# A two-layer transformer block on one core: feed-forward rests of two steps together, keys before queries at the start, normalised tokens written by GpSimd

## The chip, the cores and the metric

The kernel runs on one core of a Trainium2 chip. The core has a matrix engine (TensorE; PE for its matmuls and PEld for its weight loads in the profile), VectorE (DVE), ScalarE (ACT), GpSimd (POOL) and SyncE (SP), which here only issues DMAs. Each engine works through its own instructions in order and waits on semaphores for the others. Matmuls write PSUM, of which a core has eight banks of 128 rows by 512 float32; TensorE, VectorE and ScalarE reach PSUM here, and GpSimd works in SBUF.

The metric is the device time of one execution in microseconds (us). The kernel before takes 3205.06 us, the median of three runs (3204.47 to 3205.57).

## The reference

Two layers of the same form work on `x`, 4 batch elements of 512 tokens with 320 features, all in float32. Each layer has self-attention, attention to a context of 1601 tokens with 192 features, and a gated feed-forward, each with a layer norm ahead of it and a residual sum behind it:

```
def _ln(x, g, b):
    m = jnp.mean(x, axis=-1, keepdims=True)
    v = jnp.mean(jnp.square(x - m), axis=-1, keepdims=True)
    return (x - m) * jax.lax.rsqrt(v + EPS) * g + b
...
h1 = _ln(x, n1_g, n1_b)
x = _attn(h1, h1, q1, k1, v1, o1_w, o1_b, heads) + x
h2 = _ln(x, n2_g, n2_b)
x = _attn(h2, context, q2, k2, v2, o2_w, o2_b, heads) + x
h3 = _ln(x, n3_g, n3_b)
proj = h3 @ ff_w1 + ff_b1
a, g = jnp.split(proj, 2, axis=-1)
ff = a * jax.nn.gelu(g, approximate=False) @ ff_w2 + ff_b2
return ff + x
```

Attention has 20 heads of 16 features. The feed-forward's inner width is 1280, so `ff_w1` has 2560 columns: 1280 for `a`, 1280 for the gate `g`.

## The kernel before

**Units.** The work is a list of 88 units, in this order for each layer: 20 units of self-attention (4 batch elements times 5 groups of 4 heads), 20 of attention to the context, and 4 of feed-forward (one a batch element). Scores are computed turned, keys on partitions and 512 queries along the free dimension (`st`, line 1074); ScalarE takes the exponential (L1080); a second matmul multiplies by values and a column of ones (`av`, L1094). ScalarE copies that to SBUF (`vo`, L1110) and GpSimd adds it to the group's sum `o` (L1111). Each unit's softmax needs a maximum per query and head first; that is taken one unit ahead, by matmuls into `sps` (L903) and reduces on VectorE (`nmax`, `pm`, L919). Maxima are turned and sent by eight small DMAs into spare rows of the queries (`max_end`, L974).

**What sets the order.** The program is written out by hand in one order, which each engine keeps. Beside the fixed loops there are chains of small pieces of work ("norm", "proj", "values", "project" and others), each with an estimated cost, a due round and conditions. In every round a planner (`steps`, `pick`, `pace`) takes pieces whose turn has come and places them behind the fixed work of that round. `run(chain)` places the next piece of a chain at once, and `until(test, chain)` places pieces until something holds.

**Layer norm.** `add_norm` is a chain of pieces. Statistics are taken on VectorE (L468, L469). A reciprocal root is found by a guess and three refinements on tiny tiles, on VectorE while `start["on"]` holds, which is at the first norm alone, and on GpSimd afterwards (L438, L445 to L448). `normalise(t)` writes (x - mean) * root for one tile of 128 tokens into `hn` (L484): 320 elements a row and, ahead of a feed-forward, 64 more as a second instruction. At least one round later `turn(k)` transposes `hn` with TensorE (`hps`, L497), ScalarE writes `hT` with scale and bias, and GpSimd adds the next residual's bias to `x` (L510). There are 24 norms; 23 come after the start.

**Projections.** A self-attention unit has one piece of queries (`qps`, L699) and one of keys (`kps`, L725), 24 short matmuls each. For the first unit, ScalarE and VectorE write the result straight from PSUM into slots of 32 rows (L641, L643). For later ones ScalarE copies it (L711, L737) and GpSimd writes the slots (L647), four instructions a piece. Values (`vps`, L830) are made in eight pieces for a batch element, four of 128 columns and four of 192.

**PSUM.** `ps_st` has four single banks (tag `st`), `ps_m` two pairs of banks (tag `m`). A tile of a pool waits until an earlier tile's readers are done.

**Feed-forward.** `ff_main` (L1170) goes through ten chunks of 128 inner features, two chunks a step, five steps (c = 0, 2, 4, 6, 8). For each chunk there is a bank for `a` (from `ps_st`) and one for the gate (a half of a `ps_m` tile). The contraction over 320 is split in two of 128 rows, `full` (L1194), and a rest of 64, `rest` (L1206). The rests of `a` use rows 0 to 63 of the array and those of the gate rows 64 to 127. A float32 matmul appears as two PE instructions. At the end of a step, `gate` has ScalarE take the gelu (L1212) and VectorE the product into `hid` (L1213). `beside` gives maxima of the next unit and planned pieces their place ahead of a step and in its middle. After the five steps, `yps` (L1233) multiplies by `ff_w2`, and VectorE adds to `x`.

**Start.** Lines 1353 to 1388 load `x` and the first weights, make the first norm, project units 0 and 1, and then take the maxima of unit 0 in four rounds with pieces of values between them.

Of the kernel before, what the change touches and what calls it, by code (L numbers as in the profile page):

```python
# [66 lines left out]
def kernel(ctx: ExitStack, tc: tile.TileContext, x, context, ws, out):  # L67
# [285 lines left out]
    def add(chain, cost, f, due, ready=yes, soon=yes):  # L353
        chains[chain].append((cost if isinstance(cost, tuple) else (cost,), due, ready, soon, f))
# [69 lines left out]
    def until(test, name):  # L424
        while not test():
            assert chains[name], name
            run(name)
# [31 lines left out]
    def add_norm(l, b, i, put, done, due):  # L459
        xb = xs[b]  # L460
        s = {}

        def stats(t):
            if t == 0:
                hn_used.append(b)
                s["mv"] = two.tile([P, NQ, 2], F32, tag="mv", name="mv")
            st = three.tile([P, 6], F32, tag="st6", name="st6")
            nc.vector.bn_stats(st, xb[:, t, :])  # L468
            nc.vector.bn_aggr(s["mv"][:, t, :], st)  # L469

        def root(step):
            if step == 0:
                s["root"] = guess_root(s["mv"][:, :, 1])
                s["rstd"] = s["root"][1]
            for _ in range(step + 1):
                better_root(*s["root"])
            s["round"] = clock["round"]

        def normalise(t):
            if t == 0:  # L480
                s["hn"] = one.tile([P, NQ, D + REST], F32, tag="hn", name="hn")

            for to, at, n in ((0, 0, D), (D, D - REST, REST))[: 1 + i // 2]:
                nc.vector.tensor_scalar(  # L484
                    s["hn"][:, t, to : to + n], xb[:, t, at : at + n],
                    s["mv"][:, t, 0:1], s["rstd"][:, t : t + 1], ALU.subtract, ALU.mult,
                )
            s["round"] = clock["round"]

        def turn(k, at, n):  # L490
            if k == 0:
                s["hT"] = two.tile([P, 3, N], F32, tag="hT", name="hT")
                readers.append(done)
            ps = step_bank([P, N], "hps")
            n += REST if n == REST else 0
            for t in range(NQ):
                nc.tensor.transpose(ps[:n, t * P : (t + 1) * P], s["hn"][:, t, at : at + n], ident)  # L497
            if start["on"] and k == 1:
                nc.vector.tensor_scalar(
                    s["hT"][:n, k, :], ps[:n, :],  # L500
                    lng[i][:n, k : k + 1], lnb[i][:n, k : k + 1], ALU.mult, ALU.add,
                )
            else:
                nc.scalar.activation(
                    s["hT"][:n, k, :], ps[:n, :], AF.Identity,
                    bias=lnb[i][:n, k : k + 1], scale=lng[i][:n, k : k + 1],
                )
            for t in ((0,), (1,), (2, 3))[k]:

                nc.gpsimd.tensor_tensor(xb[:, t, :], xb[:, t, :], brow[(3 * l + i) % 2], ALU.add)  # L510
            if k == 2:
                hn_used.pop()
                put(s["hT"])

        for t in range(NQ):
            add(
                "norm", LIGHT, lambda t=t: stats(t), due - 22 + t,
                (lambda: stage[b] == 3 * l + i and not hn_used and b in loaded) if t == 0 else yes,
                (lambda: b == 0 or clock["round"] >= loaded[b] + 5) if t == 0 else yes,
            )  # L520
        for step in range(2):
            add(
                "norm", 0.0 if step else LIGHT, lambda step=step: root(step), due - 18 + step, yes,
                (lambda: clock["round"] > s["round"]) if step else yes,
            )
        for t in range(NQ):
            add(
                "norm", LIGHT, lambda t=t: normalise(t), due - 13 + t, yes,
                (lambda: clock["round"] >= s["round"] + 1) if t == 0 else yes,
            )  # L530
        for k, at, n in (DK if i < 2 else FK + [(2, 2 * P, REST)]):
            add(
                "norm", 0.58, lambda k=k, at=at, n=n: turn(k, at, n), due - 6 + 2 * k,
                may_overwrite if k == 0 else yes, lambda: clock["round"] >= s["round"] + 1,
            )
# [113 lines left out]
    def add_proj(u):  # L649
# [145 lines left out]
                add(chain, (0.05 + 0.427 / parts,) * 3, lambda part=part: queries(part), due - 2, unread)  # L795

        if not u.cross:
            add_queries()
            add(chain, (0.477,) * 3, keys, due, free)
        else:  # L800
            add(chain, 2.45, keys_of_context, keys_due, free)
            add_queries()
            for _ in range(HG):
                add(
                    "slots", 0.0, lambda: u.kslots and u.kslots.popleft()(), keys_due,
                    lambda: u.keyed, lambda: clock["slots"] > 0,
                )
# [362 lines left out]
    def ff_main(u, give, nxt):  # L1170
        done = 0

        def beside(room, n):

            nonlocal done
            if room:
                for extra in give(done, True)[1]:
                    round_of([], extra)
            done += n
            if done == u.steps - 1 and nxt is not None and nxt.kind != "ff":  # L1180
                max_reduce(nxt)
                max_end(nxt)
            steps(True)
            for _ in range(n - 1):
                steps(False)

        hc = one.tile([P, 6, N], F32, tag="ctxT", name="hid")
        hid = [hc[:, i, :] for i in range(6)]

        hid += [kbuf[1][:, i * N : (i + 1) * N] for i in range(3)] + [kbuf[2][:, :N]]  # L1190

        def full(c, i, ps):
            for k, at, n in FK:
                nc.tensor.matmul(  # L1194
                    ps,
                    lhsT=w1[:, k, i * FF + c * P : i * FF + (c + 1) * P],
                    rhs=u.hT[:, k, :],
                    start=(k == 0),
                    stop=False,
                )  # L1200
            return ps

        def rest(c, pss):
            for i, ps in enumerate(pss):
                rows = slice(i * REST, (i + 1) * REST)
                nc.tensor.matmul(  # L1206
                    ps, lhsT=w1r[rows, c * P : (c + 1) * P], rhs=u.hT[rows, 2, :], start=False, stop=True
                )

        def gate(c, pss):  # L1210
            gl = prs.tile([P, N], F32, tag="pr", name="gl")
            nc.scalar.activation(gl, pss[1], AF.Gelu, bias=b1[:, NHC + c : NHC + c + 1])  # L1212
            nc.vector.scalar_tensor_tensor(hid[c], pss[0], b1[:, c : c + 1], gl, ALU.add, ALU.mult)  # L1213

        for c in range(0, NHC, 2):

            beside(True, 2)
            gates = ps_m.tile([P, 2, 512], F32, tag="m", name="fps")
            pss = []
            for i in range(2):  # L1220
                if i:
                    beside(False, 2)
                ps = ps_st.tile([P, 512], F32, tag="st", name="fps")
                pss.append([full(c + i, 0, ps), full(c + i, 1, gates[:, i])])
            for i in range(2):
                rest(c + i, pss[i])
            for i in range(2):
                gate(c + i, pss[i])
        ff_read.append(u)
        for t in range(NQ):  # L1230
            ps = ps_st.tile([P, 512], F32, tag="st", name="yps")
            for c in range(NHC):
                nc.tensor.matmul(  # L1233
                    ps[:, :D],
                    lhsT=hid[c][:, t * P : (t + 1) * P],
                    rhs=w2[:, c, :],
                    start=(c == 0),
                    stop=(c == NHC - 1),
                )
            nc.vector.tensor_tensor(xs[u.b][:, t, :], ps[:, :D], xs[u.b][:, t, :], ALU.add)  # L1240
            if u.l == L - 1:
                dma(out=out[u.b, t * P : (t + 1) * P, :], in_=xs[u.b][:, t, :])
            beside(True, 1)
        after(u)
# [113 lines left out]
    add_norms(0)  # L1358
    add_proj(units[0])
    warm(5)  # L1360
    add_proj(units[1])
    until(lambda: not chains["proj"], "proj")
    add_values(units[0])
    add_proj(units[2])
    first = units[0]
    first.pairs = max_pairs(first)
    start["both"] = True
    while left(first):
        round_of([], first.pairs[0].popleft() + first.pairs[1].popleft())
        if left(first):  # L1370
            run("values")

    run("proj")
    run("values")
# [8 lines left out]
    start["on"] = start["both"] = False  # L1383
    run("proj")

    for _ in range(3):
        run("values")
    clock["credit"] = 0.0

# [45 lines left out]
```

## Time and profile before

| | |
|---|---|
| median of three runs | 3205.06 us |
| the profiled execution's own time | 3204.68 us |
| its span, first to last instruction | 3202.9 us |
| TensorE matmuls busy | 3167.7 us (99%) |
| VectorE busy | 2068.9 us (65%) |
| ScalarE busy | 1972.4 us (62%) |
| GpSimd busy | 1202.3 us (38%) |
| the first feed-forward, four units | from about 1330 to 1608 us |
| the second feed-forward, four units | from about 2920 to 3200 us |
| writes of `hn` on VectorE (L484) | 128, 65.1 us together |
| granted TensorE clock, mean | 0.999 of full speed |

A group's line names the source line, engine, operation, output and inputs and the shape, then the count; behind the first bar its busy time and the mean duration in ns; behind the second the idle time of the engine ahead of it and what ended most of that. A timeline's line has start and duration in us, engine, line, operation, tiles and count, and in brackets the idle time ahead of it with what ended it. The chain of waits follows the work that ended last back to the beginning. Matmuls overlap and their ends are modelled, so the starts of two blocks tell more than a block's own length.

### The profile page before, as it was taken

How to read it: one execution, taken by the hardware profiler on the slowest of the kernel's cores; microseconds unless marked ns; L12 is line 12 of the kernel's file. 1: busy time of each engine (PE TensorE's matmuls, PEld its weight loads, DVE VectorE, ACT ScalarE, POOL GpSimd, SP SyncE). 2: the span in 40 equal slices, each digit the busy share in tenths (PEclk: the TensorE clock that was granted, in tenths of full speed). 3: DMA queues.
4: the chain of work that ended last, by engine and by line, in shares of the span. 5: the costliest groups of instructions: out<-in, count | busy, mean ns of one | idle time of the engine just before them, and what ended most of it. 6: DMA issues, size and time to landing. Idle time of an engine off the chain costs nothing. (4 is left out here: it accounts for less than half of the span.)

```text
span 3202.9 us, 81370 instructions
## 1 busy us (share of the span) xinstructions
PE 3167.7 (99%) x33970; PEld 1462.6 (46%) x33970; DVE 2068.9 (65%) x2663; ACT 1972.4 (62%) x3951; POOL 1202.3 (38%) x1617
## 2 busy tenths in 40 slices
PE   8999999999999999999999999999999999999999
PEld 3444444444444444354444444444444444443555
DVE  7787778778678677422247777777777777773221
ACT  4666577777777777611146665778778777785110
POOL 5555334443443443201125553344444444432000
PEclk9999999999999999999999999999999999999999
DMA  2220011100100100100012100110010010001000
GB/s 66 56 70 17 14 27 38 33 21 20 32 21 21 31 16 11 39 6 0 1 30 61 34 14 14 24 27 16 16 32 9 16 32 11 14 10 37 9 11 15
DMA packets 104851, 77.84 MB, mean 24 GB/s; under 512 B 42908, under 2 KB 95012, under 8 KB 104484
## 3 DMA queue, kind: packets, MB, share of 16 engines
q1 hardware_dynamic: 104400, 72.63, 9.2%
q8 instruction: 268, 4.39, 0.6%
q14 instruction: 99, 0.81, 0.1%
q0 software_dynamic: 64, 0.00, 0.0%
q10 hardware_dynamic: 20, 0.00, 0.0%
HBM read 33.04 MB, written 7.93 MB: 13 GB/s over the span
## 5 line engine op out<-in xcount | busy, mean ns | idle before, releaser
L1080 ACT ACTIVATE pr<-st 128x512 f32<-128x512 f32 (+1 forms) x2720 | 1408.8, 602 | 430.1 <-PE sps L903 366.4
L1074 PE MATMUL st<-q,kT 32*128 32x512 f32 (+1 forms) x5440 | 1363.3, 614 | 3.8 <-DVE nmax L919 1.5
L919 DVE TENSOR_REDUCE pm<-sps 128x2 f32<-128x1024 f32 (+1 forms) x974 | 1133.9, 1203 | 269.0 <-PE sps L903 262.7
L903 PE MATMUL sps<-kT,q 32*128 32x512 f32 x5120 | 1273.6, 620 | 14.3 <-DVE nmax L919 11.3
L1111 POOL TENSOR_TENSOR o<-o,vo 128x512 f32<-128x512 f32 x576 | 734.3, 1275 | 1373.1 <-ACT vo L1110 1201.8
L1074 PEld LDWEIGHTS st<-q,kT 32*128 32x128 f32 (+1 forms) x5440 | 504.0, 181 | 520.0 <-ACT pr L1080 291.7
L1094 PE MATMUL av<-pr,vals 128*32 128x512 f32 (+1 forms) x5440 | 729.3, 605 | 0.2
L919 DVE TENSOR_REDUCE nmax<-sps 128x2 f32<-128x1024 f32 (+1 forms) x339 | 378.2, 1156 | 148.0 <-PE sps L903 145.9
L903 PEld LDWEIGHTS sps<-kT,q 32*128 32x128 f32 x5120 | 405.3, 183 | 125.9 <-issue 81.4
L1110 ACT COPY vo<-av 128x512 f32<-128x512 f32 x576 | 339.7, 590 | 45.5 <-PE av L1094 41.4
L1094 PEld LDWEIGHTS av<-pr,vals 128*32 128x32 f32 (+1 forms) x5440 | 110.0, 108 | 493.3 <-ACT pr L1080 480.1
L1194 PE MATMUL fps<-hT,w 128*128 128x512 f32 x640 | 288.2, 599 | 1.9 <-DVE hid L1213 1.9
L1212 ACT ACTIVATE gl<-fps,b 128x512 f32<-128x512 f32 x80 | 50.7, 684 | 386.7 <-PE fps L1206 386.7
L647 POOL TENSOR_SCALAR q<-qst,keep,zero 64x128 f32<-64x128 f32 (+1 forms) x476 | 231.1, 486 | 59.9 <-ACT qst L711 26.7
L1194 PEld LDWEIGHTS fps<-hT,w 128*128 128x128 f32 x640 | 117.4, 190 | 148.8 <-issue 142.4
L438 POOL TENSOR_SCALAR root<-root 128x4 f32<-128x4 f32 x23 | 5.3, 231 | 332.7 <-DVE root L432 332.2
L1213 DVE SCALAR_TENSOR_TENSOR hid<-fps,b,gl 128x512 f32<-128x512 f32 x48 | 33.8, 746 | 147.5 <-ACT gl L1212 147.5
L1021 PEld LDWEIGHTS ops<-wo,aT 112*32 112x32 f32 (+1 forms) x3072 | 97.8, 110 | 68.3 <-issue 37.1
L699 PE MATMUL qps<-hT,wq 112*32 112x128 f32 (+3 forms) x2880 | 125.5, 308 | 0.5 <-DVE pm L919 0.5
L1021 PE MATMUL ops<-wo,aT 112*32 112x160 f32 (+1 forms) x3072 | 125.2, 300 | 0.2
L699 PEld LDWEIGHTS qps<-hT,wq 112*32 112x32 f32 (+1 forms) x2880 | 86.3, 110 | 79.1 <-issue 38.9
L1240 DVE TENSOR_TENSOR x<-yps,x 128x320 f32<-128x320 f32 x32 | 15.7, 491 | 146.5 <-PE yps L1233 146.5
(88 smaller groups left out, 2259.6 us busy)
## 6 DMA issues: line engine op xcount, KB each, us to landing
kT<-kst SPq DMA_DIRECT2D x320, 48.0 KB
aT<-o SPq DMA_DIRECT2D x320, 32.0 KB
q<-turned SPq DMA_DIRECT2D x636, 1.0 KB
w<-in_L_xattn_ff_w_dram SPq DMA_DIRECT2D x20, 256.0 KB
ctxT<-ctxT SPq DMA_DIRECT2D x24, 208.0 KB
ctxT<-ctxT SPq DMA_DIRECT2D x12, 416.0 KB
ctxin<-in_ctx_dram SPq DMA_DIRECT2D x24, 192.0 KB
w<-in_L_xattn_ff_w_dram SPq DMA_DIRECT2D x20, 160.0 KB
```

Source lines behind the costliest of these rows:

```text
L647: nc.gpsimd.tensor_scalar(to, stage[rows, :w], keep[b][rows], more[rows], ALU.mult, ALU.add)
L699: nc.tensor.matmul(ps[to, :w], lhsT=wq[:n, k, gs], rhs=first.hT[:n, k, at[i] : at[i] + w], start=(k == 0), stop=(k == 2),)
L903: nc.tensor.matmul(ps, lhsT=u.q[j * SLOT : (j + 1) * SLOT, t * P : (t + 1) * P], rhs=u.kT[j * SLOT : (j + 1) * SLOT, u.k0 + s * 512 : u.k0 ...
L919: nc.vector.tensor_reduce(to[:, j : j + n], part, AX.X, ALU.max, negate=(ns == 1))
L1021: nc.tensor.matmul(ps[f : f + m, : D // 2], lhsT=aT[:n, k, t * P + f : t * P + f + m], rhs=wo[:n, k, cols], start=(k == 0), stop=(k == 2),)
L1074: nc.tensor.matmul(st[:r, :], lhsT=u.kT[rows, u.k0 + u.cols[c] : u.k0 + u.cols[c] + r], rhs=u.q[rows, :], start=True, stop=True)
L1080: nc.scalar.activation(p[:r], st[:r], AF.Exp)
L1094: nc.tensor.matmul(ps[i * SLOT : (i + 1) * SLOT, :], lhsT=columns_of[:r, head : head + SLOT], rhs=pr.pop((c, j))[:r, :], start=True, stop= ...
L1110: nc.scalar.copy(vo, ps)
L1111: nc.gpsimd.tensor_tensor(u.o, u.o, vo, ALU.add)
L1194: nc.tensor.matmul(ps, lhsT=w1[:, k, i * FF + c * P : i * FF + (c + 1) * P], rhs=u.hT[:, k, :], start=(k == 0), stop=False,)
L1212: nc.scalar.activation(gl, pss[1], AF.Gelu, bias=b1[:, NHC + c : NHC + c + 1])
```

## The change

There are three parts.

*Feed-forward.* `full` now does both contractions of both banks of a chunk; `rests` does the four rests of a step. In steps 0, 4 and 8 the rests follow the full matmuls, as before. Behind the rests of steps 0 and 4, the banks of the next step (2 and 6) are taken at once and that step's rests are placed there, as the first contribution to those banks. In steps 2 and 6 the full matmuls then add to banks already begun, and no rests follow. `beside` is called in the same order and with the same arguments as before. Both `ps_st` banks of a step are now taken together.

*Start.* For unit 0 the keys are placed ahead of the queries. Unit 1's projections are no longer placed ahead of the rounds of maxima but behind the first and second of them; values follow behind the third. Four pieces of values instead of three come after the start, so six in all instead of seven are placed ahead of the main loop.

*Normalised tokens.* `normalise` uses GpSimd unless `start["on"]` holds, so 23 of the 24 norms.

```diff
-                nc.vector.tensor_scalar(
+                (nc.vector if start["on"] else nc.gpsimd).tensor_scalar(
                     s["hn"][:, t, to : to + n], xb[:, t, at : at + n],
...
         if not u.cross:
-            add_queries()
+            if u.i:
+                add_queries()
             add(chain, (0.477,) * 3, keys, due, free)
+            if not u.i:
+                add_queries()
...
-        def rest(c, pss):
+        def full(c, pss, ahead):
+
             for i, ps in enumerate(pss):
-                rows = slice(i * REST, (i + 1) * REST)
-                nc.tensor.matmul(
-                    ps, lhsT=w1r[rows, c * P : (c + 1) * P], rhs=u.hT[rows, 2, :], start=False, stop=True
-                )
+                for k, at, n in FK:
+                    nc.tensor.matmul(
+                        ps,
+                        lhsT=w1[:, k, i * FF + c * P : i * FF + (c + 1) * P],
+                        rhs=u.hT[:, k, :],
+                        start=ahead and k == 0,
+                        stop=not ahead and k == 1,
+                    )
+
+        def rests(c, pss, ahead):
+
+            for e in range(2):
+                for i, ps in enumerate(pss[e]):
+                    rows = slice(i * REST, (i + 1) * REST)
+                    nc.tensor.matmul(
+                        ps,
+                        lhsT=w1r[rows, (c + e) * P : (c + e + 1) * P],
+                        rhs=u.hT[rows, 2, :],
+                        start=ahead,
+                        stop=not ahead,
+                    )
...
+        def banks():
+            gates = ps_m.tile([P, 2, 512], F32, tag="m", name="fps")
+            return [[ps_st.tile([P, 512], F32, tag="st", name="fps"), gates[:, e]] for e in range(2)]
+
+        pss = None
         for c in range(0, NHC, 2):
...
+            ahead = pss is not None
+            if not ahead:
+                beside(True, 2)
+                pss = banks()
+
+            for e in range(2):
+                if e or ahead:
+                    beside(ahead and not e, 2)
+                full(c + e, pss[e], not ahead)
+            these, pss = pss, None
+            if not ahead:
+                rests(c, these, False)
+                if c + 2 < NHC:
+                    pss = banks()
+                    rests(c + 2, pss, True)
+            for e in range(2):
+                gate(c + e, these[e])
...
     warm(5)
+    until(lambda: not chains["proj"], "proj")
     add_proj(units[1])
-    until(lambda: not chains["proj"], "proj")
     add_values(units[0])
...
-    while left(first):
+    for chain in ("proj", "proj", "values", None):
         round_of([], first.pairs[0].popleft() + first.pairs[1].popleft())
-        if left(first):
-            run("values")
+        if chain:
+            run(chain)
...
-    for _ in range(3):
+    for _ in range(4):
         run("values")
```

More of the change, by code (lines that the diff above doesn't have):

```diff
@@ L1190, in ff_main @@
         hid += [kbuf[1][:, i * N : (i + 1) * N] for i in range(3)] + [kbuf[2][:, :N]]
[L1192 to L1199, printed above, removed]
-                )
-            return ps
-        def rest(c, pss):
-            for i, ps in enumerate(pss):
-                rows = slice(i * REST, (i + 1) * REST)
-                nc.tensor.matmul(
-                    ps, lhsT=w1r[rows, c * P : (c + 1) * P], rhs=u.hT[rows, 2, :], start=False, stop=True
-                )
+        def full(c, pss, ahead):
+            for i, ps in enumerate(pss):
+                for k, at, n in FK:
[17 more added lines that the diff above has]
+                    )
         def gate(c, pss):
@@ L1213, in gate @@
             nc.vector.scalar_tensor_tensor(hid[c], pss[0], b1[:, c : c + 1], gl, ALU.add, ALU.mult)
+        def banks():
+            gates = ps_m.tile([P, 2, 512], F32, tag="m", name="fps")
+            return [[ps_st.tile([P, 512], F32, tag="st", name="fps"), gates[:, e]] for e in range(2)]
+        pss = None
         for c in range(0, NHC, 2):
[L1217 to L1228, printed above, removed]
+            ahead = pss is not None
[14 more added lines that the diff above has]
+                gate(c + e, these[e])
         ff_read.append(u)
```

## The prediction

> **What bounds the kernel now.** I read the page first: its engine shares, its slices, its chain of waits and its groups.
>
> ```profile
> span 3202.9 us, 81370 instructions
> PE 3167.7 (99%) x33970; PEld 1462.6 (46%) x33970; DVE 2068.9 (65%) x2663; ACT 1972.4 (62%) x3951; POOL 1202.3 (38%) x1617
> ...
> PE 25%; DVE 0%; POOL 0%; ACT 0%; issue 0%; ACTq 0%; DVEq 0%
> ```
>
> From the list of groups, the line that the change moves to another engine:
>
> ```profile
> L484 DVE TENSOR_SCALAR hn<-x,mv,root 128x320 f32<-128x320 f32 (+1 forms) x128 | 65.1, 547 | 15.5 <-POOL root L448 15.3
> ```
>
> The reader is to see that TensorE is busy from end to end and that the chain holds almost nothing else; work taken off VectorE counts only where TensorE waits for VectorE. The list of waits shows how rarely: TensorE's `sps` matmuls waited 11.3 us for `nmax` and 2.7 for `pm`. So a gain must be TensorE time. The merged chain, in order of time, shows the last feed-forward unit (starts, then durations in us):
>
> ```profile
> 3133.02 6.87 PE fps L1194 x16
> 3139.88 1.92 PE fps L1206 x8
> 3141.80 7.06 PE fps L1194 x16
> 3148.86 1.92 PE fps L1206 x8
> ```
>
> Sixteen full matmuls take 6.87 us after `yps` (also 128 rows high) and 7.06 after the 64-row rests: entering 128-row work from another height costs 0.2. Single full matmuls follow each other by 0.43 (the timeline's weight loads: 3.43 per 8). Two rests run at once, on rows 0 to 63 and 64 to 127, so eight should take 4 x 0.43 = 1.72; they take 1.92, another 0.2. Rests are thus already side by side in pairs; what is left is 0.2 per change of height.
>
> Next, the timeline of TensorE and VectorE around one pair of steps with other work between:
>
> ```profile
> 2947.27 1.99 PE L1206 MATMUL fps<-hT,w1r 64*128 64x512 f32 x8
> ...
> 2949.19 1.09 PE L497 MATMUL hps<-ident,hn 128*128 128x128 f32 x8
> 2949.39 1.27 ACT L1212 ACTIVATE gl<-fps,b 128x512 f32<-128x512 f32 x2 [9.82 <-PE fps L1206]
> 2950.11 1.41 DVE L1213 SCALAR_TENSOR_TENSOR hid<-fps,b,gl 128x512 f32<-128x512 f32 x2 [5.27 <-ACT gl L1212]
> ...
> 2950.92 3.70 PE L1194 MATMUL fps<-hT,w 128*128 128x512 f32 x8 [0.64 <-DVE hid L1213]
> ```
>
> Counted from the rests' start, gelu begins at +2.12, the two products end at about +3.6 and +4.25, and the next full matmul waits until +3.65 for the bank that the first product frees: the oldest of the four is taken.
>
> **The feed-forward.** Per unit five groups of rests become three: steps (0, 2) and (4, 6) share one, step 8 keeps its own: two mergers a unit, 16 in all. Each removes one entry into 64-row height (0.2) and the later return to 128 rows (0.2), unless 32-row work (`ops`, `sps`) follows there and needs its own entry. Counts of instructions stay. In the timeline, 32-row work follows step 2 or 6 at both places in the first unit of each layer, once in layer 0's second, and at both of layer 0's last: 7 of 16. So 9 x 0.4 + 7 x 0.2 = 5.0 us.
>
> The merger holds four small banks across the next step's start; that step's other work gets the two that step c's products free. The second four rests end at +3.43, plus 0.2 for a change of height, 3.63. One early transpose or projection then finds the bank freed (3.65): nothing. A second waits to 4.27. Three places have two transposes there (1358.8, 1434.2, 2949.2). Before, the fulls after them start at +3.65 with rests still to come; after, at 4.27 + 0.44 = 4.71 with the rests done: a 1.92 block less, 1.06 later, so 0.86, of which 0.2 or 0.4 is counted above: about 1.6 us for the three. In layer 0's last unit, `sps` and `kps` come there. `sps` takes both freed banks, and `kps` (at 1559.9 and 1585.1, now +3.6) must wait for VectorE: products to 4.25, a reduce of 1.2 and one of 0.6, so about +6.1. The step pair goes from 15.64 to 16.2: 0.6 lost at each, where 0.2 gained was counted, so -1.6. Together 5.0 us, bounds 2.5 and 7.
>
> **The start.** Keys, then queries of unit 0 leave by the same alternating ACT/DVE line of eight pieces (13.21 to 17.28). The first `sps` at 17.34 waited for the last, a piece of keys; with keys first it needs only the sixth (queries' first half), 1.2 us sooner. Unit 1's projections (1.5 us each on TensorE) move from 14.3 to 17.0, where TensorE waited anyway, into the gaps between rounds, in place of values of 0.87. A round is bound by reduces at 2.45, and 1.14 + 1.5 = 2.64 overruns it twice, 0.25 each. The last reduce, its transpose and the eight issues of `q<-turned` on SP, ACT and POOL move up 0.7. POOL still issues its two behind the 2.5 us of unit 2's slots (30.41); unit 1's slots, 5 us of POOL, come 1.4 later and end before. Of seven values, six are left; the other (1.18) falls after 34, where TensorE waits for reduces up to 0.75 at a time. Gain 0.7, bounds 0 and 1.2. The planner's later choices may shift by an item of work: 1.5 either way.
>
> **The normalised tokens.** 23 norms, 92 writes of 320 elements and 32 of 64, leave VectorE. No row has them on GpSimd. Nearest are its tensor-scalars with per-row operands:
>
> ```profile
> L647 POOL TENSOR_SCALAR q<-qst,keep,zero 64x128 f32<-64x128 f32 x320 | 143.8, 449 | 23.0
> L647 POOL TENSOR_SCALAR kT<-kst,keep,ones 64x256 f32<-64x256 f32 x156 | 87.6, 561 | 36.9 <-ACT kst L737 23.8
> ...
> L510 POOL TENSOR_TENSOR x<-x,brow 128x320 f32<-128x320 f32 x96 | 84.0, 893 | 62.2 <-DVE hn L484 52.1 <-DMA brow<-in_L_xattn_o_b_dram 8.2
> ```
>
> Slope 0.87 ns an element: 0.62 at 320, 0.39 at 64, so 92 x 0.62 + 32 x 0.39 = 70 us on an engine at 38%. I take 0.62; ends 0.56 (256 elements) and 0.89 (two inputs). What queues behind: `o` sums, slots of `q` and `kT`, `x + brow`. Laid onto GpSimd's timeline behind the sum of the same round, the writes push `o` by at most 0.6 us and slots by 0.7, which are read rounds later; `x + brow` by up to 3.7, hidden by the rounds before the next statistics. The root is on GpSimd already, so the hand-over that VectorE waited for (15.3) goes.
>
> Who waits is the first transpose. It has 1.1 to 12 us after the last write in attention, and GpSimd would start a write up to 5.3 later than VectorE did (2.7 in the norms with less than 2). Only at 78.5 is it late: the `o` sum ends at 78.53, two writes at 79.8, so 1.1. At 1315 and 2905, where TensorE stood at the write already, eight writes from 2901.8 end near 2905.9: 0.4 each. Loss 1.9. At 0.89 a write they become 1.6 and twice 1.5, 4.6.
>
> Against that, VectorE's write was long where it met GpSimd's sum:
>
> ```profile
> 2382.17 1.28 POOL L1111 TENSOR_TENSOR o<-o,vo 128x512 f32<-128x512 f32 x1
> 2382.25 1.73 DVE L484 TENSOR_SCALAR hn<-x,mv,root 128x320 f32<-128x320 f32 x2 [0.69 <-POOL root L448]
> 2383.91 2.34 DVE L919 TENSOR_REDUCE pm<-sps 128x2 f32<-128x1024 f32 x2
> ```
>
> The first of the two writes took 1.38 where 0.44 is usual, the reduce behind it came late, and `kps` at 2385.17 waited 0.9 for it. The like at 2617.96 costs 0.4; at 801 and 1039 `kps` waits for `ctxT` behind one and two writes, 0.3 and 0.6; near 1633 perhaps 0.3. Gain 2.5, net 0.6, bounds -2 and 3. Were the cover gone, every late microsecond would fall on TensorE's transposes.
>
> [...] The rows here say 0.62 to 0.44, a factor of 1.4. [...]
>
> **Sum.** 5.0 + 0.7 + 0.6 = 6.3. The profiled execution took 3204.68 (1.8 around its span), 0.4 under the median of 3205.06; from the median, 3198.8.
>
> **Rivals.** (1) The mergers don't save the returns: the drain between heights is paid in the rests' second half, or other work stands at more junctions. Only entries count, 16 x 0.2 = 3.2, less 1.6 for layer 0's last unit; with the rest 1.3: 3202.2. For it: 7 of 16 places have such work. Against: 6.87 after `yps`. (2) VectorE's relief is worth more. TensorE's waits for `nmax` and `pm` come to 14 us; if a third of what isn't near a write shortens as well, 4 more: 3195. Against: most lie at 298 to 400 and 1900 to 2000, with no write there. (3) Slower: two free banks are too few, because the bank taken is the last freed. Then the fulls of step c + 4 wait for the product of the pair just ended, 0.2 + 0.69 + 0.75 = 1.65 us, at 16 places: 26 us, 3225. Against: 2950.92 shows the oldest taken. From 0.4 us a place it eats the gain.
>
> **How the numbers follow.** Mine 0.58, rival 1 0.20, rival 2 0.16, rival 3 0.06. About 0.2% (6.4 us) is what a measurement can tell: the border is 3198.65, in the middle of my case (3196.5 to 3201). Half of mine and rival 2 are faster: 0.45; the other half and rival 1 same: 0.49. The range takes in half of rival 2 and rival 1 with the bad ends of its terms: 3195 to 3203.5.
>
> **What would show it.** Per feed-forward unit two blocks of 16 rest instructions (3.6 us) and one of 8; fulls after such pairs 6.87. `hn` on POOL near 0.62; `hps` waiting for it at about 78, 1315 and 2905 alone. First `sps` near 16.2, first `st` near 33.1. It is wrong if fulls or steps wait for `hid` longer than 0.8, or if `hps` waits for `hn` in many norms.

## The result and the profile after

The kernel after takes 3211.75 us (median of ten runs, 3210.23 to 3215.01), the kernel before 3205.22 in ten runs beside it (3204.47 to 3210.42). The ratio is 1.0019, with a 95% interval of 1.0011 to 1.0028: slower by 6.5 us where 6.3 of gain was forecast. The profiled execution took 3215.01 (span 3213.2), 3.3 above the median. One thing varies from execution to execution, and it is told below: where TensorE's granted clock falls to one half.

The page first: TensorE's busy time is shorter by 1.7 us, the span longer by 10.3, and GpSimd, which had 0% of the chain of waits, has 2% of it (the chain that could be followed covers some 67% of the span here, 25% before).

```profile
span 3213.2 us, 81419 instructions
PE 3166.0 (99%) x33970; PEld 1465.4 (46%) x33970; DVE 2010.3 (63%) x2539; ACT 1973.3 (61%) x3951; POOL 1348.1 (42%) x1741
...
PE 63%; POOL 2%; DVE 2%; issue 0%; ACT 0%; DMA 0%; SPq 0%; DVEq 0%; POOLq 0%; ACTq 0%
```

The groups with their shapes kept apart answer the line that the change moved. The columns behind the bar are busy time and the mean of one in ns.

```profile
L647 POOL TENSOR_SCALAR q<-qst,keep,zero 64x128 f32<-64x128 f32 x320 | 144.6, 452 | 23.0
L484 POOL TENSOR_SCALAR hn<-x,mv,root 128x320 f32<-128x320 f32 x92 | 132.4, 1442 | 1.9
...
L647 POOL TENSOR_SCALAR kT<-kst,keep,ones 64x256 f32<-64x256 f32 x156 | 87.1, 558 | 41.8 <-ACT kst L737 28.7
...
L484 POOL TENSOR_SCALAR hn<-x,mv,root 128x64 f32<-128x64 f32 x32 | 18.6, 582 | 0.0
...
L484 DVE TENSOR_SCALAR hn<-x,mv,root 128x320 f32<-128x320 f32 x4 | 1.5, 443 | 0.0
```

A write of 320 elements takes 1442 ns on GpSimd, not 620; the first norm's four, still on VectorE, take 443 (547 was VectorE's mean before, with writes that met GpSimd's sums). From 64 to 320 elements the slope is (1442 - 582) / 256 = 3.36 ns an element, where the slots of `q` and `kT` have (558 - 452) / 128 = 0.83. GpSimd is loaded with 151 us of these writes where 70 was put.

The list of waits (total, times, longest) has a new pair of lines; before, no transpose waited for GpSimd:

```profile
PEld hps L497 <- POOL hn L484: 19.0, 16, 1.8
...
PE hps L497 <- POOL hn L484: 13.5, 12, 1.6
```

The timeline at one of these places, the norm at 2157 us:

```profile
2156.47 1.28 POOL L1114 TENSOR_TENSOR o<-o,vo 128x512 f32<-128x512 f32 x1
...
2157.45 0.43 PE L497 MATMUL hps<-ident,hn 128*112 128x128 f32 x2
2157.73 2.85 POOL L484 TENSOR_SCALAR hn<-x,mv,root 128x320 f32<-128x320 f32 x2
...
2159.22 0.32 PE L497 MATMUL hps<-ident,hn 128*112 128x128 f32 x1 [1.34 <-POOL hn L484]
...
2160.64 1.32 PE L497 MATMUL hps<-ident,hn 128*112 128x128 f32 x5 [1.09 <-POOL hn L484]
```

Two of the four writes are behind an `o` sum, so the third and fourth transposes stand 1.34 and 1.09 us. That is not the whole price. The windows around it (length, busy time of PE, PEld, DVE, ACT and POOL, then the granted clock):

```profile
2157.00:2160.00 3.00, 1.20 (x11) 0.32 (x3) 1.08 (x1) 1.26 (x3) 3.00 (x3) 1.00 0.49 143
2160.00:2163.00 3.00, 2.36 (x13) 1.52 (x17) 0.00 (x0) 1.55 (x2) 3.00 (x4) 0.51 0.00 0
2163.00:2166.00 3.00, 3.00 (x20) 0.79 (x16) 1.42 (x2) 1.38 (x3) 0.46 (x1) 0.50 0.00 0
```

Behind the stall TensorE runs at half clock: in the trace's clock record for 6.83 us from 2160.04, and likewise for 6.83 from 1316.95 and 3.41 from 2917.80. At the 0.50 and 0.51 of these windows up to half of such a stretch is lost by my estimate, so up to 3.4 us at each of the first two places, more than the two stalls here together (2.43).

The feed-forward shows what the prediction said. The merged chain in its last unit (starts, then durations):

```profile
3144.09 6.87 PE fps L1199 x16
3150.95 3.63 PE fps L1212 x16
3154.59 13.93 PE fps L1199 x32
3168.52 3.63 PE fps L1212 x16
```

Sixteen rests in 3.63 us where two blocks of 1.92 stood, and 6.87 + 7.06 for the fulls on both sides of a step boundary without rests.

### The profile page after: what moved, and what is told of

It is laid out like the page before. It is cut to its first block, busy times and chain, and to the rows that moved or that the text cites. A ratio compares the mean times of both kernels' runs of the same rounds, so it can differ in the third digit from the quotient of the medians.

```text
span 3213.2 us, 81419 instructions
## 1 busy us (share of the span) xinstructions
PE 3166.0 (99%) x33970; PEld 1465.4 (46%) x33970; DVE 2010.3 (63%) x2539; ACT 1973.3 (61%) x3951; POOL 1348.1 (42%) x1741
## 4 chain that ended last, share of the span: by engine, by line
PE 63%; POOL 2%; DVE 2%; issue 0%; ACT 0%; DMA 0%; SPq 0%; DVEq 0%; POOLq 0%; ACTq 0%
PE st L1077 16%; PE av L1097 13%; PE sps L906 8%; PE fps L1199 8%; PE yps L1253 5%; PE fps L1212 2%; PE ops L1024 2%; PE kps L755 2%; PE vps L851 2%; PE qps L699 2%; POOL hn L484 1%; PE sps L930 1%; PE vps L833 1%; PE hps L497 1%; PE kps L725 1%; DVE nmax L922 1%
## 5 line engine op out<-in xcount | busy, mean ns | idle before, releaser
L906 PE MATMUL sps<-kT,q 32*128 32x512 f32 x5120 | 1275.3, 621 | 15.0 <-DVE nmax L922 10.4
L647 POOL TENSOR_SCALAR q<-qst,keep,zero 64x128 f32<-64x128 f32 (+1 forms) x476 | 231.7, 487 | 69.5 <-ACT qst L711 36.3
L484 POOL TENSOR_SCALAR hn<-x,mv,root 128x320 f32<-128x320 f32 x124 | 149.9, 1220 | 1.9
```

The lines of the kernel that those rows point to most:

```text
L484: (nc.vector if start["on"] else nc.gpsimd).tensor_scalar(s["hn"][:, t, to : to + n], xb[:, t, at : at + n], s["mv"][:, t, 0:1], s["rstd"] ...
L647: nc.gpsimd.tensor_scalar(to, stage[rows, :w], keep[b][rows], more[rows], ALU.mult, ALU.add)
L906: nc.tensor.matmul(ps, lhsT=u.q[j * SLOT : (j + 1) * SLOT, t * P : (t + 1) * P], rhs=u.kT[j * SLOT : (j + 1) * SLOT, u.k0 + s * 512 : u.k0 ...
```

## The experiments

To say where time goes between two kernels I set the starts of the same units in the two traces against each other (the first copy of a unit's `av`, or a feed-forward's sums into `x`); "between 513 and 557" below is such a difference. The times of the kernel before in these comparisons are its medians beside the same runs; they lie between 3204.6 and 3206.1, so a difference between kernels that ran beside different ones is good to about 1.5 us.

**The parts one by one.** My theory after the result (A): GpSimd's writes lose the time, the rest gains as forecast. The rival (B): the feed-forward loses, through keys that wait for VectorE in layer 0's last unit.

Feed-forward and start as after, all normalised tokens on VectorE:

```diff
-                (nc.vector if start["on"] else nc.gpsimd).tensor_scalar(
+                nc.vector.tensor_scalar(
```

> The kernel after, with the normalised tokens written by VectorE throughout, as before. Theory A (GpSimd's writes of the normalised tokens are what lost the time: 1.44 us each in the profile after, where 0.62 was put): without them the gains of the other two parts stand, 3205.2 - 5.0 - 0.7, so 3199.5, between 3197.5 and 3202; no transpose waits for the normalised tokens longer than before. Theory B (the feed-forward loses, because keys and transposes beside the merged rests wait for VectorE and the clock falls behind those waits): 3205 or more, with the waits of 1.49 us for keys in layer 0's last unit still there.

Measured 3200.83 against 3206.07: ratio 0.9984 (0.9976 to 0.9993).

The kernel before with only this line the other way:

```diff
-                nc.vector.tensor_scalar(
+                (nc.vector if start["on"] else nc.gpsimd).tensor_scalar(
```

> The kernel before, with only the writes of the normalised tokens moved to GpSimd. Theory A: all of the loss and the gain that it hides, 3205.2 + 6.5 + 5.7 = 3217, between 3214 and 3220; granted clock at one half behind the long waits of the transposes near 1316, 2160 and 2917. Theory B: the move alone costs little, 3205 to 3209. My prediction's step alone (net gain 0.6): 3204.6.

Measured 3216.65 against 3206.07: 1.0032 (1.0020 to 1.0045), 10.6 us slower.

The kernel before with only the new feed-forward (`full`, `rests`, `banks` and the loop over steps, as in the diff):

> The kernel before, with only the feed-forward changed. The prediction's step: 5.0 us gained, 3200.2, bounds 2.5 to 7. Theory A lets it be 3200 to 3202: the waits of 1.49 us for keys at two places of layer 0's last unit, with 3.4 us at half clock behind one of them (1.7 us), cost 1 to 2 more than predicted. Theory B: 3205 or more.

Measured 3203.45 against 3206.07: 0.9991 (0.9982 to 0.9999).

The kernel before with only the new start (keys before queries for unit 0, the rounds as in the diff):

> The kernel before, with only the start changed (keys of the first group ahead of its queries, the projections and values between the rounds in another order). The prediction's step: 0.7 us gained, 3204.5, bounds 0 to 1.2, planner shift 1.5 either way. Rival: the wait of 1.9 us near 16 us, followed by 3.4 us at half clock in the profile after, takes the gain back: 3205.5 to 3206.5.

Measured 3204.54 against 3206.07: 0.9995 (0.9986 to 1.0004); by its time alone this can't be told from no change.

So A holds: +0.32% for the writes, -0.09% and -0.05% for the others make +0.18%, and +0.19% was measured. But B holds in part as well: of a forecast 5.0 us the feed-forward alone gave 2.6. Its loss is where the prediction had put a small one, in layer 0's last unit; that unit is 5.6 us longer than before in the trace of the kernel with feed-forward and start. Its timeline:

```profile
1555.49 1.41 DVE L1223 SCALAR_TENSOR_TENSOR hid<-fps,b,gl 128x512 f32<-128x512 f32 x2 [13.61 <-ACT gl L1222]
1556.35 1.73 PE L906 MATMUL sps<-kT,q 32*128 32x512 f32 x8
1557.52 2.42 DVE L922 TENSOR_REDUCE nmax<-sps 128x2 f32<-128x1024 f32 x3 [0.62 <-PE sps L906]
1559.40 1.55 PE L725 MATMUL kps<-hT,wk 112*32 112x256 f32 x24 [1.32 <-DVE nmax L922]
```

and its windows, with the granted clock as the number behind the five engines:

```profile
1557.00:1560.00 3.00, 1.68 (x20) 0.67 (x18) 2.48 (x4) 0.00 (x0) 0.00 (x0) 1.00 0.00 0
1560.00:1564.00 4.00, 4.00 (x24) 1.78 (x13) 0.53 (x2) 0.37 (x1) 2.21 (x4) 0.59 0.01 4
```

`sps` takes both banks that the products free, and `kps` stands 1.32 us for the reduce, twice in the unit; behind each stall the clock record has 3.41 us at one half. By the same estimate, half of twice 3.41, the clock makes 3.4 of the 5.6, and the two stalls the other 2.2.

**Feed-forward without merging in that unit**, normalised tokens on VectorE, start as after:

```diff
-                if c + 2 < NHC:
+                if c + 2 < NHC and (nxt is None or nxt.kind == "ff"):
```

> Feed-forward and start as in the kernel after, the normalised tokens on VectorE throughout, and in the unit of feed-forward that comes last in layer 0 no rests of the next step are moved up (they run as in the kernel before), so that its keys don't wait for VectorE. In the trace with the rests moved up, that unit was 5.6 us longer than in the kernel before. If the waits of 1.3 us for keys and the stretches at half clock behind them are what it lost: 3200.8 - 5.6 = 3195.2, between 3194 and 3197. If the loss there is of another kind and comes back elsewhere: 3199 to 3201.

Measured 3197.95 against 3204.69: 0.9976 (0.9967 to 0.9985). The unit is back at its old length (the trace reaches its end 4.8 us ahead of the kernel before, as it reached its beginning), and the seven others gained 1.07, 1.27, 0.80 in layer 0 and 1.07, 0.80, 0.75, 0.79 in layer 1. The time is 1 us above the range I gave, so the 5.6 of the one profiled execution is not all found again in the medians: where the clock falls differs from execution to execution. That the unit loses by the merging is shown; how much on average is not: the two medians differ by 2.9 us, the two traces at this unit by 5.6.

**Why a write takes 1.44 us.** The same values with another pair of operations, `x * root + less`:

```diff
+                nc.gpsimd.tensor_tensor(s["less"], s["mv"][:, :, 0], s["rstd"], ALU.mult)
+                nc.gpsimd.tensor_scalar(s["less"], s["less"], -1.0, None, ALU.mult)
...
-                    s["mv"][:, t, 0:1], s["rstd"][:, t : t + 1], ALU.subtract, ALU.mult,
+                    s["rstd"][:, t : t + 1], s["less"][:, t : t + 1], ALU.mult, ALU.add,
```

> The kernel after, but GpSimd writes the normalised tokens as x * root + less, with less = -mean * root made by two operations on 128x4 a norm, so that the write has the pair of operations (mult, add) that the slots of queries and keys have (L647). If the pair (subtract, mult) is what makes the write 1.44 us where the slots' slope gave 0.62: about 0.62 a write of 320 and 0.4 of 64, hardly a wait of the transposes, and the relief of VectorE without the loss: 3194, between 3191 and 3199. If the length comes from 128 rows in place of 64, or from the place of the operands: writes stay near 1.44, and the time 3211 to 3214.

Measured 3191.72 against 3204.69: 0.9960 (0.9946 to 0.9975). The groups:

```profile
L494 POOL TENSOR_SCALAR hn<-x,root,less 128x320 f32<-128x320 f32 x92 | 56.0, 611 | 1.9
...
L494 POOL TENSOR_SCALAR hn<-x,root,less 128x64 f32<-128x64 f32 x32 | 12.6, 393 | 0.0
```

611 and 393 ns, where the prediction took 620 and 390. So the count of rows and the operands were rightly read from the slots' line; the pair of operations was not looked at (L647 multiplies and adds). The last question on it is whether subtract is slow in itself or only in first place. With `x * root - mean * root`:

```diff
-                nc.gpsimd.tensor_scalar(s["less"], s["less"], -1.0, None, ALU.mult)
...
-                        s["rstd"][:, t : t + 1], s["less"][:, t : t + 1], ALU.mult, ALU.add,
+                        s["rstd"][:, t : t + 1], s["less"][:, t : t + 1], ALU.mult, ALU.subtract,
```

> As the kernel with (mult, add), but with the pair (mult, subtract): x * root - mean * root, so that the term needs no change of sign and one small operation a norm falls away. If it is the operation subtract that is slow on GpSimd, in either place: writes of about 1.4 us and 3208 to 3213. If only subtract as the first operation is slow, or the order of the two operands: about 0.61 a write and 3189 to 3193.

One run, 3215.26, above the 3208 to 3213 put, and the group:

```profile
L493 POOL TENSOR_SCALAR hn<-x,root,less 128x320 f32<-128x320 f32 x92 | 132.1, 1439 | 1.9
```

Subtract is slow on GpSimd in either place: 1442 ns as the first operation and 1439 as the second, against 611 for (mult, add). Why was not tried.

**Whether the half clock comes from the stall.** Five short matmuls of the identity with itself ahead of the third and the fourth transpose of three norms; the transposes overwrite what they write:

```diff
+                if k == 0 and t >= 2 and (l, i, b) in ((0, 2, 0), (1, 2, 0), (1, 1, 1)):
+                    for _ in range(5):
+                        nc.tensor.matmul(
+                            ps[:n, t * P : (t + 1) * P], lhsT=ident[:, :n], rhs=ident, start=True, stop=True
+                        )
```

> The kernel after, with five short matmuls of the identity with itself ahead of the third and the fourth transpose of the three norms whose transposes stand still longest (near 1316, 2160 and 2917 us); each five take some 1.1 us of the time in which TensorE stood waiting for GpSimd's write, and the transposes overwrite what they wrote. If the half clock behind these waits comes from TensorE standing still: the granted clock stays at 1 there, and of 6.83 + 6.83 + 3.41 us at half clock half is saved, 8.5 less up to 2 where the five outlast the wait: 3203 to 3206. If the clock falls for another reason: 3211 to 3214, with the same stretches at half clock.

Measured 3207.95 against 3204.69: 1.0008 (0.9999 to 1.0016), 3.8 under the kernel after's own median. Its timeline and windows at the place shown above, which here comes 1.87 us sooner:

```profile
2155.58 0.43 PE L502 MATMUL hps<-ident,hn 128*112 128x128 f32 x2
...
2155.85 1.25 PE L499 MATMUL hps<-ident 128*112 128x128 f32 x10
...
2157.35 0.32 PE L502 MATMUL hps<-ident,hn 128*112 128x128 f32 x1 [0.24 <-POOL hn L484]
...
2157.51 1.26 PE L499 MATMUL hps<-ident 128*112 128x128 f32 x10
```

```profile
2155.00:2158.00 3.00, 2.76 (x26) 1.97 (x19) 1.23 (x2) 1.39 (x3) 3.00 (x3) 1.00 0.51 143
2158.00:2161.00 3.00, 3.00 (x26) 2.07 (x27) 0.28 (x1) 1.83 (x3) 3.00 (x4) 1.00 0.00 0
```

The writes are as late as before, but the clock stays at 1.00, where it was 0.51 and 0.50 behind the stalls at this place, and the three places are 2.7, 2.7 and 1.7 us shorter in the trace. At these places, TensorE standing still is what halves its clock. The mean granted clock of all runs points the same way: 0.997 to 0.999 in eleven runs of this kernel, 0.995 to 0.997 in ten of the kernel after. The two traces are 6.3 us apart and the medians 3.8, so the share of the median that this accounts for is less certain. The kernel with the writes alone on GpSimd tells the stall's own price from the clock's: near 2157 it has the same two stalls (1.34 and 1.09 us) and no half clock behind them, and its unit lost 1.6 us against the kernel before, where the kernel after lost 4.3 against the same kernel with VectorE's writes. The time missed its range by 2 us: in the profiled execution half clock still stands at four places (17, 802, 1038, 1591) where the kernel after's profile had three besides the mended ones (16, 802, 1566).

**Whether lateness is all that hurts.** Slow writes kept, but the first transpose at the earliest five rounds after the last write:

```diff
-                may_overwrite if k == 0 else yes, lambda: clock["round"] >= s["round"] + 1,
+                may_overwrite if k == 0 else yes, lambda: clock["round"] >= s["round"] + 5,
```

> The kernel after, with its slow writes of 1.44 us kept, but the first transpose of a norm may come at the earliest five rounds after the last write, not one. If the writes hurt only because the transposes come before their end: no wait of transposes, no half clock near 1317, 2160 and 2918, and the time of the kernel with the writes on VectorE less its relief: 3194 to 3201. If GpSimd's load itself hurts, by late sums and slots, or the later transposes put other work late: 3205 or more.

Measured 3202.86 against 3204.57: 0.9990 (0.9981 to 0.9999), between the two cases. Of the 16 weight loads of transposes that waited for GpSimd's `hn` (19.0 us), two are left (1.7 us); no transpose itself waits for it any more, there is no half clock near the three places, and 8.9 us against the kernel after came back. But half clock of 3.41 us still stands at five places (17, 567, 1041, 1587 and 1881). Two of them stand beside waits that the kernel after has not there: 2.57 us for VectorE's `ctxT` (until 566.81) and 1.27 us for GpSimd's slots of `kT` (until 1879.12). The planner puts many other pieces elsewhere, so what remains can't be put down to one cause from this run.

**What VectorE's relief is worth.** The kernel before with the normalised tokens on GpSimd by (mult, add), and nothing else of the change:

```diff
-                nc.vector.tensor_scalar(
+                nc.gpsimd.tensor_scalar(
                     s["hn"][:, t, to : to + n], xb[:, t, at : at + n],
-                    s["mv"][:, t, 0:1], s["rstd"][:, t : t + 1], ALU.subtract, ALU.mult,
+                    s["rstd"][:, t : t + 1], s["less"][:, t : t + 1], ALU.mult, ALU.add,
```

(VectorE and the old pair stay while `start["on"]` holds, and `less` is made as above.)

> The kernel before, with only the normalised tokens moved to GpSimd, and written there as (mult, add) at the 0.61 us that this pair took. The prediction's step had a net gain of 0.6 at 0.62 a write, between -2 and 3: 3205. If VectorE's relief is worth as much as the trace of the two kernels with the new feed-forward says (12.2 us between them unit by unit, of which some 2 to 4 lie in where the half clock fell): 3195 to 3198.

Measured 3194.21 against 3204.57: 0.9965 (0.9952 to 0.9977), a gain of 10.4 us from a step that the prediction priced at 0.6. The timeline of VectorE and of the `av` matmuls in the kernel before shows one place of it:

```profile
1731.67 0.25 DVE L993 RECIPROCAL rd<-oturn 128x16 f32<-128x16 f32 x1
...
1732.89 0.45 DVE L484 TENSOR_SCALAR hn<-x,mv,root 128x320 f32<-128x320 f32 x1 [0.97 <-POOL root L448]
1733.23 1.07 PE L1094 MATMUL av<-pr,vals 128*32 128x512 f32 x8
1733.26 0.21 DVE L967 STREAM_TRANSPOSE turned<-nmax 128x32 f32<-128x32 f32 x1
1733.39 2.31 DVE L919 TENSOR_REDUCE nmax<-sps 128x2 f32<-128x1024 f32 x2
...
1735.62 1.07 DVE L997 TENSOR_TENSOR oturn<-oturn,rd 128x256 f32<-128x256 f32 x1
...
1736.82 0.64 PE L1094 MATMUL av<-pr,vals 128*32 128x512 f32 x4
```

and the same place in this kernel:

```profile
1725.76 2.36 DVE L929 TENSOR_REDUCE nmax<-sps 128x2 f32<-128x1024 f32 x2 [0.31 <-PE sps L913]
...
1726.43 1.07 PE L1104 MATMUL av<-pr,vals 128*32 128x512 f32 x8
1726.71 0.61 POOL L494 TENSOR_SCALAR hn<-x,root,less 128x320 f32<-128x320 f32 x1
...
1728.04 0.42 DVE L1007 TENSOR_TENSOR oturn<-oturn,rd 128x256 f32<-128x256 f32 x1
...
1729.38 1.07 PE L1104 MATMUL av<-pr,vals 128*32 128x512 f32 x8
```

In the kernel before VectorE stood 0.97 us at the head of its queue for GpSimd's root, then wrote, and two reduces stood behind. They begin 0.16 after the `av` of that round instead of 0.67 ahead of it, the product behind them meets GpSimd's `o` sum (1.07 in place of 0.42), and the round from `av` to `av` takes 3.59 us in place of 2.95. No listed wait of TensorE shows that here: `sps` and `st`, each on 32 rows, run side by side. In the kernel before, `sps` begins 0.40 us behind `st` in that round (1734.63, just after the first reduce has ended, and 1734.23), and the two blocks of 0.70 us overlap by 0.30; in this kernel they begin at 1727.44 and 1727.43 and overlap for all but 0.01 of their 0.70. TensorE is busy with `st` meanwhile, and the round only becomes longer. VectorE stood so at seven norms in attention (0.96 near 132, 0.58 near 220, 0.38 near 1024, 0.97 near 1733 and 1821, 0.69 near 2382 and 2615); the units around them gained 0.96, 0.35, 0.97, 0.96, 0.96, 1.27 and 1.60, together 7.1. The other 10 us of the 15.3 that VectorE waited for the root lie at three norms beside feed-forward, whose units gained nothing. Six more gains of 0.4 to 1.3 have no such wait. At three of them writes were long beside GpSimd's sums (two took 1.80 at 544.61 and at 2145.51, one 1.33 at 782.65); near 801 and 1039 `kps` came sooner because `ctxT` no longer stands behind a write, as the prediction had it, with 1.0 and 0.8 in place of 0.3 and 0.6. The sixth, 0.45 near 590, stays open. That the wait ahead of the write, and not the write's own time, makes most of the relief is read from timelines; no run took one away without the other.

**Slow writes only where that relief lay.** Feed-forward and start as in the kernel without merging in layer 0's last unit, with

```diff
-                nc.vector.tensor_scalar(
+                (nc.gpsimd if i == 1 and (l, b) != (1, 1) else nc.vector).tensor_scalar(
```

> As the one without rests moved up in layer 0's last unit of feed-forward, but GpSimd writes the normalised tokens of the norms ahead of attention to the context, save that of the second batch element in layer 1; VectorE all others. Unit by unit, the kernel after gained 5.4 us in layer 0's attention to the context over the same kernel with the writes on VectorE, and 2.8 in layer 1's outside that norm. If these gains are VectorE's relief from writes that met GpSimd's sums: 3195.2 - 8.2 = 3187, between 3185 and 3190. If they are chance of the planner's order: 3194 to 3197.

Measured 3192.25 against 3204.69: 0.9959 (0.9944 to 0.9973), 5.7 us under the same kernel with all writes on VectorE, not 8.2. The relief is there even with slow writes, if no transpose comes soon after; its size was taken too high, in part because the comparison that it came from counted a stretch of half clock in the other trace (3.41 us at 1038, so 1.7 by the estimate of half) as relief.

**Both losses mended**, (mult, add) and no merging in layer 0's last unit:

> The kernel with GpSimd's write as (mult, add), and in the unit of feed-forward that comes last in layer 0 no rests moved up. If the two losses are independent: 3191.7 less the 3 to 5.6 us that the second mending was worth with the writes on VectorE: 3186 to 3189. If GpSimd's writes had already changed the order in that unit so that little is left to mend: 3190 to 3192.

Measured 3185.80 against 3205.63: ratio 0.9934 (0.9921 to 0.9948), 19.8 us faster than before and 26 faster than the kernel after, 0.2 below the range. The second mending was worth more here, 5.9 us between the medians where it was 2.9 with the writes on VectorE: the trace with (mult, add) alone has 10.24 us at half clock in layer 0's last unit, this one has none there, and the unit is 7.2 us shorter.

## Why the prediction was wrong, by its steps

**"I take 0.62"** is the step that failed. It took GpSimd's write from the slope of L647, the same instruction with other operations; 1.44 us was measured. The upper end, 0.89, from a two-input sum, did not hold it either. With it fell "only at 78.5 is it late" and "0.4 each" at 1315 and 2905: against the same kernel with VectorE's writes the kernel after lost 3.8 near 80, 5.9 near 1316, 4.3 near 2160 and 4.9 near 2916, 1.0 at each of two more and 1.4 at a third, some 22 us where 1.9 was put. The prediction's own sign of being wrong, `hps` waiting for `hn` in many norms, stands in the list of waits with 16 weight loads.

**The price of a stall was counted once.** A late transpose was put at its own length. Behind stalls of 1.3 to 1.7 us came, at most places though not at all, 3.4 to 6.8 us at half clock. The same fault sits in the feed-forward's step for layer 0's last unit: `kps` was put at +6.1 us from the rests' start with 0.6 lost at each pair; it came at +6.7, 1.1 was lost at each, and the clock took 3.4 more in that execution by the estimate above.

**"Gain 2.5"** was far too small for a write of 0.6: 10.4 net was measured with (mult, add). The prediction quoted the 15.5 us that VectorE stood ahead of L484, wrote that this hand-over goes, and gave it no price, since TensorE's list of waits shows little for VectorE. Rival 2, more relief, was thus right in kind, though its 4 us on top were too few; in the kernel after it was hidden under the loss.

**The factor between the engines** was put at 0.62 to 0.44, so 1.4. A write with one tensor input and subtract took 1442 ns on GpSimd against 443 on VectorE, a factor of 3.3; with (mult, add) GpSimd took 611, a factor of 1.4 to the same 443. The factor thus held for (mult, add) and failed for the pair that the change kept.

**The feed-forward** was right elsewhere: blocks of 3.63, fulls of 6.87 behind fulls, fulls at 4.80 (1361.18 rests to 1365.97, and 2960.31 to 2965.11) behind two early transposes where 4.71 was put, and the seven undisturbed units gained 6.55 where the terms for them make 6.2 (5.0, less 0.4 for the last unit's two places, and 1.6). Rival 1 (entries alone) and rival 3 (fulls waiting for `hid`: 0.2 us once in all) are out.

**The start** was right in its mechanism, half wrong in its sum. The first `sps` came at 16.18 and the first `st` at 33.11, as put. Started alone, the second unit was reached 1.4 us sooner, twice the forecast. In the kernel after, TensorE stands 1.71 us for `q` there, and in six of the ten profiles with this start the clock falls to one half for 3.41 us right behind; the second `sps` then comes at 20.32 in place of 19.08, and the gain is gone. Timelines, after and then the start alone:

```profile
16.18 1.87 PE L906 MATMUL sps<-kT,q 32*128 32x512 f32 x8 [1.71 <-DVE q L641]
17.98 2.41 PE L699 MATMUL qps<-hT,wq 112*32 112x256 f32 x24
20.32 1.14 PE L906 MATMUL sps<-kT,q 32*128 32x512 f32 x8
```

```profile
16.55 1.14 PE L906 MATMUL sps<-kT,q 32*128 32x512 f32 x8 [1.71 <-DVE q L641]
17.62 1.50 PE L699 MATMUL qps<-hT,wq 112*32 112x256 f32 x24
19.08 1.14 PE L906 MATMUL sps<-kT,q 32*128 32x512 f32 x8
```

Same wait, same instructions; only the clock differs: from 15 to 18 us and from 18 to 21 the windows have 0.74 and 0.69 in the kernel after, 1.00 and 1.00 in the start alone.

## What to carry to other kernels

An operation's price on an engine belongs to its operation codes too, not to the instruction's name and shape alone (here 1439 to 1442 ns with subtract, 611 without): before moving work, write it with codes that a row of that engine already shows. Where one engine waits at the head of its queue for another, price everything queued behind it, even if the bounding engine's list of waits is empty; lengths of rounds show it (3.59 us against 2.95 around a wait of 0.97). And on this TensorE, busy for 99% of the span, stalls of 1.3 to 1.7 us were followed at most places by 3.41 or 6.83 us at a clock of 0.50, so tenths gained at sixteen places were lost by three stalls.

## What the runs showed of the hardware

Subtract in a tensor-scalar on GpSimd took 1439 to 1442 ns for 128x320 float32, (mult, add) 611.

The half clock (0.50 in the windows) came in stretches of 3.41 us or twice that, save where a record ends, and a stall of 1.3 to 1.7 us was enough for one, though not always. In each of the fourteen clock records, every change of the clock lies a whole number of 3.413 us behind the first one (3, 4, 233, 234, 384, 386 and so on in the kernel after; 233, 234 and 936 in the kernel before). So each record can be divided into intervals of 3.413 us, and a stall set against them. Near 2157 the same two stalls lie mostly in one interval in the kernel after, and the clock fell at its end; with the writes alone on GpSimd an edge lies between them, and it did not fall. The interval after, then the two of the other (busy time of PE is the second number):

```profile
2156.63:2160.04 3.41, 1.57 (x11) 0.32 (x3) 1.46 (x2) 1.63 (x4) 3.41 (x3) 1.00 0.43 126
...
2154.53:2157.94 3.41, 2.07 (x15) 0.48 (x11) 1.96 (x2) 2.13 (x5) 3.41 (x4) 1.00 0.41 123
2157.94:2161.35 3.41, 2.32 (x18) 1.50 (x21) 0.37 (x1) 1.92 (x3) 3.41 (x4) 1.00 0.01 3
```

At the start, the stall of 1.71 us lies whole in one interval in all six profiles where the clock falls; in three of the four others an edge cuts it. The fourth, the start alone, is an exception: with 1.70 us busy of 3.41, as in the kernel after, its clock did not fall. And TensorE need not stand still throughout an interval for a fall at its end: it was busy for 2.09 of the 3.41 us ahead of the fall at 1560.72 in the kernel with feed-forward and start, and of that at 1566.12 in the kernel after, while 2.07 busy, above, brought no fall. What decides it is not shown.
